# First layer of a four-layer attention kernel: two pieces of VectorE work moved to GpSimd

## The chip, the cores and the metric

The kernel runs on one core of one Trainium2 chip. The metric is the device time of one execution in microseconds (us). Engines are named as in the profile: PE is TensorE, DVE is VectorE, ACT is ScalarE, POOL is GpSimd, SP is SyncE, whose queue issues the transfers.

## The reference

Four layers run one after another on x, 8 batches of 100 rows of 512 numbers, with a context of 361 rows a batch; all in 32-bit floats. Layer 1, which the change touches, is cross-attention with grouped keys, then a residual and a norm:

```python
scores = jnp.einsum('bkgld,bksd->bkgls', q, k) * scale
attn = jax.nn.softmax(scores + mask, axis=-1)
out = out @ Wo + bo
x = out + hidden_state
return (x - mu) * jax.lax.rsqrt(var + EPS) * gamma + beta
```

Layer 2 is a recurrent mixing block that begins with a norm of x. Layer 3 is a plain attention. Layer 4 has two attentions of 16 heads of 128 columns, each with one added key `bias_k` and value `bias_v`, and a two-matrix network. The second piece of work that the change touches belongs to layer 4: the kernel does not score the added key against every query, but forms, for each head h, the product of `wq[h]` (512x128) with the row `bias_k[h] - bk[h]`. That gives a 512-vector a head, and depends on weights alone.

## The kernel before, in words

Layer 1 works through the batches b = 0 to 7 (loop from line 452). A batch has 8 x 4 x 100 rows of scores, cut into 7 row tiles t for each of 4 groups of heads. One pass of the inner loop, a *step* here, is one t: score matmuls (`scores`, L326), negated row maximum on DVE (`softmaxed`, L338), exponential on ACT (L342), transposes on PE (`turned`, L350) of the tile before, and their copies out of PSUM (`evict0`): three on ACT (L230), one on DVE (L232). In this layer the instructions of PE, DVE and ACT run in the order in which the program writes them (`manual_schedule`); those of POOL and SP are ordered by the compiler's scheduler.

Into the steps other work is woven by generators, of which `advance()` (L426) lets each go on to its next `yield` once a step:

- `values` (L378) multiplies a batch's probabilities by its values, projects them with Wo and adds the residual (L413 on POOL, L414 on DVE), then takes the row statistics (`stats`, L101 and L102).
- `finish` (L358) is the layer's end norm. It runs for the groups of batches 0 to 3, 4 and 5, and 6 and 7, when the last of a group is ready: square root on ACT (L365), reciprocal on DVE (L366), then for each batch two DVE operations (L371, L372) in one step and the statistics for layer 2 in the next. For the second and third group it also takes the square root for layer 2 (`next_ones`, L361 and L362): of batches 0 to 3, and 4 to 7. Group three runs after the loop (`while steps: advance()`, L502), with nothing else left in the layer.
- `prepare` (L143), once for each attention of layer 4, forms the added keys' vectors `wx`. It is not in that list but has one `next(adding, None)` a step from batch 1 on (L478), after the row maxima. In each step it loads the weights of one head (`wqx`, 256 KB) and its row spread over the partitions (`kb`, 64 KB), both in three buffers, and works on the head loaded two steps before: four multiply-and-sum operations on DVE at L172, one for each chunk of 128 rows. `wx` is first read in layer 4, at 880 us.

Layer 2 starts with transposes of the normed rows of batches 0 and 1 (L577), their eviction on ACT (`xu`, L579), differences on POOL (L588), and mixing on DVE (L596). There only PE's order is written by hand. Its tiles take memory that layer 1's tiles held, so its first constants (`first`, L525) are loaded when those are free. PE's spare time is filled with `fold_chunk` matmuls (`pf`).

Of the kernel before, what the change touches and what calls it, by code (L numbers as in the profile page):

```python
# [12 lines left out]
ALU = mybir.AluOpType  # L13
AX = mybir.AxisListType
PSUM = bass.MemoryType.PSUM

P = 128
B, L, C, S = 8, 100, 512, 361
T = B * L
NC = C // P  # L20
# [36 lines left out]
def kernel(ctx: ExitStack, tc: tile.TileContext, d: dict, out: bass.AP):  # L57
    nc = tc.nc
# [14 lines left out]
    mv = const.tile([L, B, 2], F32, tag="mv", name="mv")  # L73
    rstd = const.tile([L, B], F32, tag="rstd", name="rstd")
# [12 lines left out]
    x = [xpool.tile([L, C], F32, tag=f"x{b}", name=f"x{b}") for b in range(B)]  # L87
# [11 lines left out]
    def stats(pool, b, into=None):  # L99
        st = pool.tile([L, 6], F32, tag="bnst", name="bnst")  # L100
        nc.vector.bn_stats(st, x[b])  # L101
        nc.vector.bn_aggr((mv if into is None else into)[:, b, :], st)  # L102
# [33 lines left out]
    NH = 16  # L136
# [6 lines left out]
    def prepare(layer, tmp, into):  # L143


        wx = prep.tile([P, NC, NH], F32, tag=f"wx{layer}", name="wx")
        hv = tmp.tile([NH, 3, P], F32, tag="hv", name="hv", bufs=1)
        nc.sync.dma_start(out=hv, in_=d[f"L3_hv{layer}"])
        yield
        dk = hv[:, 0]  # L150
        nc.vector.tensor_tensor(dk, hv[:, 0], hv[:, 1], ALU.subtract)
        dkd = folded.tile([NH, P], F32, tag=f"dk{layer}", name="dkd")
        nc.sync.dma_start(out=dkd, in_=dk)
        nc.vector.tensor_tensor(hv[:, 1], dk, hv[:, 2], ALU.mult)
        ch = prep.tile([NH, 1], F32, tag=f"ch{layer}", name="ch")
        nc.vector.tensor_reduce(ch, hv[:, 1], AX.X, ALU.add)
        dv = prep.tile([P, NH], F32, tag=f"dv{layer}", name="dv")
        at, bt = PV_AT[f"L3_xattn_bias_v{layer}"], PV_AT[f"L3_xattn_bv{layer}"]
        nc.vector.tensor_tensor(dv, pv[:, at : at + NH], pv[:, bt : bt + NH], ALU.subtract)
        yield  # L160
        loaded = []
        for h in range(NH + 2):
            if h < NH:
                wq = tmp.tile([P, NC, P], F32, tag="wqx", name="wqx", bufs=3)
                nc.sync.dma_start(out=wq, in_=d[f"L3_xattn_wq{layer}"][h])
                kb = tmp.tile([P, P], F32, tag="kb", name="kb", bufs=3)
                nc.sync.dma_start(out=kb, in_=dkd[h : h + 1].to_broadcast([P, P]))
                loaded.append((wq, kb))
            if h > 1:
                wq, kb = loaded[h - 2]  # L170
                for c in range(NC):
                    nc.vector.tensor_tensor_reduce(  # L172
                        out=wq[:, c], in0=wq[:, c], in1=kb, scale=1.0, scalar=0.0,
                        op0=ALU.mult, op1=ALU.add, accum_out=wx[:, c, h - 2 : h - 1],
                    )
            yield
        into[layer] = wx, ch, dv

# [23 lines left out]
    with ExitStack() as es:  # L202
# [155 lines left out]
        def finish(bs):  # L358

            def next_ones(cols):  # L360
                nc.scalar.activation(rstd1[:, cols], mv1[:, cols, 1], AF.Sqrt, bias=eps5[:L], scale=1.0)  # L361
                nc.vector.reciprocal(rstd1[:, cols], rstd1[:, cols])  # L362

            cols = slice(bs[0], bs[-1] + 1)
            nc.scalar.activation(rstd[:, cols], mv[:, cols, 1], AF.Sqrt, bias=eps6[:L], scale=1.0)  # L365
            nc.vector.reciprocal(rstd[:, cols], rstd[:, cols])  # L366
            if bs == groups[1]:
                next_ones(slice(0, bs[0]))
            for b in bs:
                yield  # L370
                nc.vector.scalar_tensor_tensor(x[b], x[b], mv[:, b, 0:1], gamma, ALU.subtract, ALU.mult)  # L371
                nc.vector.scalar_tensor_tensor(x[b], x[b], rstd[:, b : b + 1], beta, ALU.mult, ALU.add)  # L372
                yield
                stats(p2, b, mv1)
            if bs == groups[2]:
                next_ones(slice(groups[1][0], bs[-1] + 1))

        def values(b, par, ats, y):  # L378
# [38 lines left out]
            for bs in groups:  # L417
                if b == bs[-1]:
                    yield from finish(bs)
# [13 lines left out]
        def added_keys():  # L433
            for layer in (1, 2):
                yield from prepare(layer, p2, added)
# [75 lines left out]
    with ExitStack() as es:  # L511
# [473 lines left out]
        with tc.manual_schedule(engines=L1_ORDERED):  # L985
# [11 lines left out]
            for n in range(NU * STEPS + 1):  # L997
                u, c, i = n // STEPS, n % STEPS // 4, n % 4
# [74 lines left out]
    with ExitStack() as es:  # L1073
# [438 lines left out]
        for n, (layer, half) in enumerate(steps):  # L1512
            wx, ch, dv = added[layer]
# [14 lines left out]
            loaded, made = [], {}  # L1528
# [253 lines left out]
```

## Time and profile before

| | |
|---|---|
| three runs | 2723.08, 2726.43, 2731.62 us; median 2726.43 |
| profiled execution: span from first to last instruction | 2722.8 us (its time is not given beside the span) |
| mean granted PE clock | 0.985 |
| busy share of the span | PE 96%, DVE 59%, POOL 38%, ACT 34% |
| layer 1, about | 0 to 311 us |
| layer 2 and 3, about | 311 to 800 us |
| layer 4, about | 800 to 2723 us |
| added keys' operations at L172 | 71.5 to 245.7 us |
| end norm at L371 and L372 | first 180.8, last 309.1 us |

A timeline line gives start, length, engine, line of the code, operation, output and inputs, shape and number. A bracket at its end is the idle time of the engine just before and what ended it. A waits line reads: engine, tile and line that waited, what it waited for, us in total, times, longest. The row of slices cuts the span into 40 equal parts; a digit is the busy share in tenths.

### The profile page before, as it was taken

Reading aid. Unit: us, or ns where it says so; the run is one execution under the profiler, and the core shown is the slowest. Engines: PE = TensorE matmul, PEld = TensorE weight load, DVE = VectorE, ACT = ScalarE, POOL = GpSimd, SP = SyncE. Lnnn points to the kernel's source line nnn. Section 1 sums busy time; section 2 is a strip of 40 time slices with the busy share of each in tenths; the row PEclk is TensorE's granted clock in tenths of the full one; section 3 lists DMA queues with packets and bytes.
Section 4 is the critical chain, followed back from the end, with each engine's and each line's share of the span. In section 5 each row is a group of like instructions: output and inputs, shape, how many; then the busy total and the mean of one; then the engine's idle time right before and its main releaser. Section 6 shows DMA issues by size and latency. Waiting matters only on the chain.

```text
span 2722.8 us, 39771 instructions
## 1 busy us (share of the span) xinstructions
PE 2609.8 (96%) x14100; PEld 2059.3 (76%) x14100; DVE 1601.2 (59%) x3987; ACT 939.2 (34%) x2143; POOL 1042.7 (38%) x1362
## 2 busy tenths in 40 slices
PE   8999889898989999999999999999999999999999
PEld 5666466676666888877789878788877788887688
DVE  4888366877524556556556556565555655654733
ACT  5777334543321333320333320243331143331211
POOL 2000144433204345455345446344446434535201
PEclk9999888999999999999999999999999999999999
DMA  7432334354214100046200034400015510005400
GB/s 230 119 104 75 115 116 124 92 145 122 81 39 151 55 23 23 4 126 169 80 23 23 1 85 145 136 16 31 12 35 151 150 43 23 23 7 168 152 13 13
DMA packets 149679, 220.58 MB, mean 81 GB/s; under 512 B 45302, under 2 KB 78646, under 8 KB 149226
## 3 DMA queue, kind: packets, MB, share of 16 engines
q1 hardware_dynamic: 149482, 218.05, 27.3%
q8 instruction: 112, 1.84, 0.3%
q14 instruction: 85, 0.70, 0.1%
HBM read 207.48 MB, written 10.53 MB: 80 GB/s over the span
## 4 chain that ended last, share of the span: by engine, by line
PE 67%; POOL 4%; DVE 3%; DMA 2%; ACT 1%; issue 1%; SPq 0%; DVEq 0%; POOLq 0%; ACTq 0%
PE pz L97 16%; PE sl L97 9%; PE pk L1175 6%; PE su L97 6%; PE pq L97 5%; PE pa L97 5%; PE po L1439 5%; PE pp L97 3%; PE pu L97 3%; PE pt L1363 2%; PE pl L97 2%; PE pl L1262 1%; DMA xin<-xd 1%; PE sc L1401 1%; PE sc L97 1%
## 5 line engine op out<-in xcount | busy, mean ns | idle before, releaser
L97 PE MATMUL pz<-at,cr 121*128 121x256 f32 (+1 forms) x960 | 255.9, 378 | 0.0
L751 POOL TENSOR_TENSOR st<-st,r 128x800 f32<-128x800 f32 x64 | 111.9, 1749 | 232.9 <-DVE st L745 198.9
L1336 DVE TENSOR_TENSOR qz<-pz,qz 128x512 f32<-128x512 f32 x192 | 131.9, 687 | 114.0 <-PE pz L97 105.8
L97 PEld LDWEIGHTS pz<-at,cr 121*128 121x128 f32 (+1 forms) x960 | 177.2, 189 | 20.8
L1175 PE MATMUL pk<-q,wb 128*128 128x400 f32 x512 | 190.2, 501 | 0.0
L97 PE MATMUL pa<-qz,wa 128*128 128x400 f32 x512 | 178.7, 500 | 0.8 <-DVE aT L1479 0.8
L97 PE MATMUL sl<-ts,ss 128*128 128x181 f32 x768 | 156.7, 326 | 3.8 <-POOL ts L1231 0.5
L97 PE MATMUL pz<-at,cs 121*128 121x256 f32 (+1 forms) x576 | 149.7, 380 | 0.0
L1248 POOL TENSOR_TENSOR ss<-qz 128x256 f32<-128x256 f32 x96 | 69.8, 727 | 203.3 <-PE su L97 115.0
L97 PEld LDWEIGHTS pa<-qz,wa 128*128 128x128 f32 x512 | 95.7, 190 | 65.9 <-DVE aT L1479 2.3
L1382 ACT ACTIVATE pr<-su,nm 128x362 f32<-128x362 f32 x96 | 54.1, 564 | 265.0 <-DVE nm L1378 264.9
L1366 ACT COPY at<-pt 121x384 f32<-121x384 f32 x192 | 84.2, 480 | 159.9 <-PE pt L1363 95.6
L1091 ACT COPY qz<-pk 128x400 f32<-128x400 f32 x128 | 63.0, 492 | 214.8 <-PE pk L1175 214.8
L97 PEld LDWEIGHTS sl<-ts,ss 128*128 128x128 f32 x768 | 118.4, 190 | 21.9 <-issue 7.1
L1175 PEld LDWEIGHTS pk<-q,wb 128*128 128x128 f32 x512 | 93.7, 190 | 45.7 <-ACT qz L1091 3.7
L745 DVE TENSOR_TENSOR_SCAN st<-wd,a 128x808 f32<-128x808 f32 x64 | 117.0, 1828 | 16.1 <-PE py L756 14.3
L350 PEld LDWEIGHTS pt<-ident,pr 115*121 115x121 f32 (+1 forms) x672 | 83.2, 185 | 56.5 <-ACT at L230 29.2
L1385 ACT ACTIVATE pr<-pr,ss 128x362 f32<-128x362 f32 x200 | 113.1, 594 | 29.1 <-DVE ss L1383 28.9
L1448 DVE TENSOR_TENSOR acc<-po,acc 128x400 f32<-128x400 f32 x196 | 111.4, 572 | 15.1 <-PE po L1439 0.5
L342 ACT ACTIVATE pr<-pr,nm 115x361 f32<-115x361 f32 (+1 forms) x224 | 115.2, 592 | 10.4 <-DVE nm L338 10.4
L97 PEld LDWEIGHTS pz<-at,cs 121*128 121x128 f32 (+1 forms) x576 | 104.4, 189 | 13.7 <-issue 1.8
L338 DVE CUSTOM_DVE_ANT_0 pr<-sc,mask 115x361 f32<-115x361 f32 (+1 forms) x224 | 106.0, 530 | 11.0 <-PE sc L326 10.4
(383 smaller groups left out, 6180.0 us busy)
## 6 DMA issues: line engine op xcount, KB each, us to landing
va<-vd SPq DMA_DIRECT2D x64, 404.0 KB
wa<-in_L_xattn_wq SPq DMA_DIRECT2D x64, 256.0 KB
wb<-in_L_xattn_wk SPq DMA_DIRECT2D x64, 256.0 KB
wa<-in_L_xattn_wv SPq DMA_DIRECT2D x64, 256.0 KB
wb<-in_L_xattn_wo SPq DMA_DIRECT2D x64, 256.0 KB
u<-pd SPq DMA_DIRECT2D x64, 200.0 KB
cr<-in_ctxR SPq DMA_DIRECT2D x16, 726.0 KB
cx<-in_ctxT SPq DMA_DIRECT2D x16, 722.0 KB
```

The source lines that it names most:

```text
L97: nc.tensor.matmul(dst, lhsT=lt, rhs=r, start=(i == 0), stop=(i == len(pairs) - 1))
L338: nc.vector.tensor_tensor_reduce(out=pr[:n], in0=sc[:n, :S], in1=mk[t][:n], scale=-1.0, scalar=FLT_MAX, op0=ALU.add, op1=ALU.min, accum_ou ...
L342: nc.scalar.activation(pr[:n], pr[:n], AF.Exp, bias=nm[:n], scale=-1.0)
L350: nc.tensor.transpose(pt[:KB, k * n : (k + 1) * n], pr[:n, lo : lo + KB], ident[:n, :n])
L745: nc.vector.tensor_tensor_scan(st.rearrange("p q b l -> p (q b l)"), wd.rearrange("p q t -> p (q t)"), a, 0.0, ALU.mult, ALU.add,)
L751: nc.gpsimd.tensor_tensor(st, st, rc.unsqueeze(1).to_broadcast([P, 4, UB, L]), ALU.mult)
L1175: nc.tensor.matmul(pk[:, :HT], lhsT=wk[:, c * P : (c + 1) * P], rhs=q, start=True, stop=True)
L1336: nc.vector.tensor_tensor(dst, pz, other, ALU.add)
L1366: nc.scalar.copy(at, pt[:KB, : 3 * TR].rearrange("p (k r) -> p k r", r=TR))
L1385: nc.scalar.activation(pr[:, : S + 1], pr[:, : S + 1], AF.Copy, scale=ss)
L1439: nc.tensor.matmul(po[:, c], lhsT=left[k][:, c * P : (c + 1) * P], rhs=right[k], start=True, stop=True)
L1448: nc.vector.tensor_tensor(acc[k], po, acc[k], ALU.add)
```

## The change

In `prepare`, POOL multiplies the whole 128 x 4 x 128 weight tile of a head by the row in one operation and folds the 128 columns to 64, 32 and 16 by additions; DVE sums the remaining 16 one step later, ahead of the next load into that buffer. So each layer's preparation takes one step more.

In `finish`, the two DVE operations of a batch become three on POOL: subtract the mean and multiply by the reciprocal deviation in one, multiply by gamma, add beta. A second `yield` leaves one step more between them and the statistics.

```diff
-        for h in range(NH + 2):
+        for h in range(NH + 3):
+            if h > 2:
+                nc.vector.tensor_reduce(wx[:, :, h - 3], loaded[h - 3][0][:, :, :16], AX.X, ALU.add)
             if h < NH:
                 wq = tmp.tile([P, NC, P], F32, tag="wqx", name="wqx", bufs=3)
                 nc.sync.dma_start(out=wq, in_=d[f"L3_xattn_wq{layer}"][h])
                 kb = tmp.tile([P, P], F32, tag="kb", name="kb", bufs=3)
                 nc.sync.dma_start(out=kb, in_=dkd[h : h + 1].to_broadcast([P, P]))
                 loaded.append((wq, kb))
-            if h > 1:
+            if 1 < h < NH + 2:
                 wq, kb = loaded[h - 2]
-                for c in range(NC):
-                    nc.vector.tensor_tensor_reduce(
-                        out=wq[:, c], in0=wq[:, c], in1=kb, scale=1.0, scalar=0.0,
-                        op0=ALU.mult, op1=ALU.add, accum_out=wx[:, c, h - 2 : h - 1],
-                    )
+                nc.gpsimd.tensor_tensor(wq, wq, kb.unsqueeze(1).to_broadcast([P, NC, P]), ALU.mult)
+                for n in (64, 32, 16):
+                    nc.gpsimd.tensor_tensor(wq[:, :, :n], wq[:, :, :n], wq[:, :, n : 2 * n], ALU.add)
             yield
...
             for b in bs:
                 yield
-                nc.vector.scalar_tensor_tensor(x[b], x[b], mv[:, b, 0:1], gamma, ALU.subtract, ALU.mult)
-                nc.vector.scalar_tensor_tensor(x[b], x[b], rstd[:, b : b + 1], beta, ALU.mult, ALU.add)
+                nc.gpsimd.tensor_scalar(
+                    x[b], x[b], mv[:, b, 0:1], rstd[:, b : b + 1], ALU.subtract, ALU.mult
+                )
+                nc.gpsimd.tensor_tensor(x[b], x[b], gamma, ALU.mult)
+                nc.gpsimd.tensor_tensor(x[b], x[b], beta, ALU.add)
+                yield
                 yield
                 stats(p2, b, mv1)
```

## The prediction

> **What bounds the kernel now.** I read the page first, for the row of slices, then the timeline of the first 320 us by batch of layer 1, then who waits for whom, then the timeline around the end of that layer.
>
> ```profile
> PE   8999889898989999999999999999999999999999
> DVE  4888366877524556556556556565555655654733
> POOL 2000144433204345455345446344446434535201
> ```
>
> One digit is 68 us. The change lies in the first four or five slices: there TensorE (PE) is at 8 or 9 tenths, VectorE (DVE) at 8 in the three in the middle, GpSimd (POOL) at nothing after the first. So there is room on GpSimd; the question is whether VectorE sets the end of anything. The busy times by stretch, cut at the start of each batch's first score matmul, say more (columns: length, PE, weight loads, DVE, ACT, POOL, granted clock, DMA share, GB/s):
>
> ```profile
> 116.50:150.90 34.40, 33.64 (x261) 22.50 (x260) 26.72 (x125) 24.37 (x56) 0.21 (x1) 1.00 0.41 117
> 150.90:186.60 35.70, 33.62 (x257) 22.41 (x256) 26.70 (x115) 27.00 (x58) 0.21 (x1) 1.00 0.33 89
> 186.60:222.00 35.40, 34.31 (x257) 22.96 (x256) 33.39 (x147) 24.40 (x55) 0.21 (x1) 1.00 0.42 118
> ```
>
> Batch 3 (first row) runs with the added keys' work inside and PE idle for 0.76 of 34.40 us. The starts of its score matmuls are 5.27, 5.21, 3.99, 6.54, 4.70, 4.60 and 4.05 us apart, and those of batches 1 and 2 the same to 0.02 us: PE's own work sets these steps, and VectorE's 26.7 us fit beside it. Only batches 4 and 5 are longer, where the end norm of batches 0 to 3 is also on VectorE. Who makes PE wait, from 40 to 250 us:
>
> ```profile
> PE pt L350 <- DVE at L232: 3.4, 6, 1.1
> PE pt L350 <- ACT at L230: 2.5, 5, 0.5
> PE pty L393 <- ACT ac L230: 0.8, 5, 0.2
> ```
>
> 3.4 us on VectorE in six waits: that is nearly all a lighter VectorE could give back here. Other stalls are hidden in matmuls that show as longer; I count those below by step lengths. At the layer's end it is different:
>
> ```profile
> 305.94 0.73 DVE L371 SCALAR_TENSOR_TENSOR x<-x,mv,gamma 100x512 f32<-100x512 f32 x1
> ...
> 309.08 0.75 DVE L372 SCALAR_TENSOR_TENSOR x<-x,rstd,beta 100x512 f32<-100x512 f32 x1
> 309.86 0.69 DVE L101 BATCH_NORM_STATS2 bnst<-x 100x6 f32<-100x512 f32 x1
> 310.59 0.18 DVE L102 BATCH_NORM_AGGREGATE mv<-bnst 100x2 f32<-100x6 f32 x1
> 310.81 0.30 ACT L361 ACTIVATE rstd<-mv,eps 100x4 f32<-100x4 f32 x1 [4.98 <-DVE mv L102]
> ...
> 311.20 1.75 ACT L579 ACTIVATE xu<-pn,pv 128x200 f32<-128x200 f32 x4
> ```
>
> This is the norm of batches 6 and 7 with nothing beside it. ScalarE (ACT) stands 4.98 us until the last statistics, takes the square root, and only then evicts layer 2's first rows (xu), which PE had finished at 305.5; PE then waits 3.21 us for xu at 312.18. The first constants of layer 2 (first, gather) are also issued only at 309.89, 0.06 us after the last use of beta. So every microsecond that this norm takes longer is late in layer 2.
>
> **The change, part by part.** *Added keys, removed:* 32 heads x 4 multiply-and-sums at L172. One is 286 ns and its read of the sum 82 ns, but they start 0.215 us apart, so 0.86 us a head, 27.5 us of VectorE in all, between 71.5 and 246 us. *Added on VectorE:* one sum of 64 elements a head. Two rows bracket it: 16 elements at 154 ns (L159) and 128 elements at 275 ns (L156); I take 0.2 us, 6.4 us in all. *Added on GpSimd:* one multiply of 512 columns (the 100x512 add of L413: 1288 ns) and folds of 256, 128 and 64 columns. 256 columns are 727 ns (L1248); the others lie between 8 columns at 248 ns (L589) and 200 at 610 ns (L1580), by the line between them 0.47 and 0.35 us. With 0.08 us between instructions, as at L1322, it is 3.1 us a head, 100 us in all, in steps that average 4.9 us. GpSimd had 0.21 us of work in a batch, so this is hidden there.
>
> What could uncover it is the ring of three buffers. Now it is load, sum, next load, once in three steps; after the change it is load, multiply and fold, sum, next load, also once in three steps. A load is issued at 96.40 (wqx) and 96.80 (kb) and the DMA share falls to 0.05 within 3 us; so the ring needs 0.2 for the sum, 0.8 for the issues, 3 for landing, 3.1 on GpSimd and about 0.3 for hand-overs (an estimate from the gaps of these rows): 7.4 us. Three neighbouring steps last at least 13.26 us (5.26, 5.22 and 2.78 in batch 6). 5.9 us are to spare, and a norm of 3.3 us ahead in GpSimd's queue fits in them too. If the cover went, the VectorE sum would wait in order ahead of the copies at L232, for which PE waits; that is the second rival.
>
> *End norm, removed:* 8 x (746 + 752 ns) of VectorE, 12 us. *Added on GpSimd:* one subtract-and-multiply and two 100x512 tensor operations a batch. The first is bounded by 679 ns (L1471, 128x400, same kind) from below and 1288 ns (L413) from above; scaled from L1471 it is 0.81. The others go by L413, eight in 9.92 us, 1.24 each. 3.3 us a batch. Each norm of batches 0 to 5 then has two steps, at least 8.0 us (2.78 + 5.22), before its statistics, so on GpSimd it is hidden; the square root that needs batches 0 to 3 comes 13 steps after the first norm, and the last of these statistics 11. No DMA is moved, and the mask loads on SP keep their places behind loads that are not late.
>
> *What the lighter VectorE gives.* I compare the steps of batches 4 to 6 with the undisturbed ones: 4.47 for 4.05; 5.35 for 5.27, 5.53 for 5.22, 6.66 for 6.54, 5.15 for 4.60; 2.97 for 2.78. Excess 0.42 + 0.08 + 0.31 + 0.12 + 0.55 + 0.19 = 1.7 us, all in steps with a norm or its statistics next to a head's sums. I count it as gained. Two more steps are long, 5.59 for 4.60 and 5.78 for 4.60; there VectorE stands 1.33 and 1.24 us for a square root for which ScalarE first loads a table (1.28 us). The change leaves that load, so these 2.2 us stay. Bounds: 0, and 1.7 + 2.2 = 3.9 us.
>
> *What the end norm costs.* Before: from 305.94 to 309.83, 3.9 us for batches 6 and 7 with the statistics of 6 between. After: GpSimd 2 x 3.3 = 6.6 us, the statistics of 6 beside it, 0.1 for crossing engines: 2.8 us later. Bounds: the lowest of all rows, 2 x (0.68 + 2 x 1.24) = 6.3, so +2.4; and GpSimd slowed as by VectorE at L648 against L834 (1879 against 1522 ns, 128x800 both), 6.6 x 1.235 = 8.15, so +4.3. Nothing hides it: xu, the constants and the fold matmuls all come after it.
>
> The Trainium skill, GPSIMD Engine Reference, section 4.1 Engine selection, speaks against this part: it says that two-input elementwise work belongs on VectorE, being about twice as slow on GpSimd, with one-input work near line rate. By twice L371 and once L371 a batch would be 0.75 + 2 x 1.49 = 3.7 us, an estimate, and the delay 3.5 instead of 2.8 us.
>
> The Trainium skill, GPSIMD Engine Reference, section 2.1 Instruction dispatch, says that the first call of a freshly loaded kernel costs about 6 us that no instruction shows; no run here shows it for this operation, whose first use would fall on batch 0's norm.
>
> *Sum.* -1.7 + 2.8 = **+1.1 us**. The profiled span is 2722.8 us, 0.3 below the shortest of the three runs (2723.08) and 3.6 below their median; no separate time of that execution is shown. From the span it would be 2723.9; against the median of 2726.43 it is 2727.5, and that is my number. A comparison of this kernel cannot tell less than about 0.3% (8.2 us) from no change, so I call it no change.
>
> **Rivals.** *One: a chain reaction in layer 2 (slower or faster).* That layer is a chain across engines; the granted clock is 0.89 from 305 to 320 us and 0.74 from 320 to 340, against 1.00 before. If PE's longer wait costs one more such 20 us stretch, 0.26 x 20 = 5.2 us come on top of 1.1; two would give +11.5, 2738. The same could go the other way: all of PE's waits in the loop (3.4 + 2.5 + 0.8 = 6.7 us) and one such stretch saved give 2714.5. For: only PE's order is fixed in that layer, and L766 takes 394 to 1912 ns by what lies beside it. Against: nearly everything in it hangs on the same late release and shifts as a whole.
>
> *Two, the slower side: GpSimd sets the ring.* It decides when landing exceeds 13.26 - 4.4 = 8.9 us, or GpSimd's share of the ring exceeds 13.26 - 4.3 = 9.0 us: then VectorE waits at each sum and a step lasts a third of the ring. At a ring of 17.6 us a step would be 5.9 instead of 4.9, and 32 steps cost +31 us: 2758. For: GpSimd in order also has a clearing at L288, which waits for VectorE once a batch. Against: the 3 us of landing, and no instruction waits for wqx or kb now.
>
> *Three: the layer's end is hidden.* If ScalarE evicts xu ahead of the last square root, the 2.8 us go and -1.7 is left: 2724.7. Against: the constants are held by beta all the same.
>
> **Chances.** Forecast (+1.1, within -1.5 and +4.3, with the runs' scatter 2720 to 2735): 0.61. Rival three: 0.09, also no change. Rival one 0.22, of it 0.09 faster by over 0.3%, 0.10 slower, 0.03 neither. Rival two 0.08, slower. Faster 0.09, same 0.73, slower 0.18. The range 2715 to 2742 takes in the forecast and both signs of rival one and leaves most of rival two and the far tails out.
>
> **What would show it.** Right: steps of batches 1 to 3 unchanged to 0.05 us; the steps of batches 4 and 5 at 5.27, 5.22, 6.54 and 4.6 but the two with table loads still long; VectorE some 33 us less busy and GpSimd some 126 us more; the last square root at L361 some 2.8 us later after the last reciprocal, and xu right behind it. Wrong: a VectorE sum that waits for GpSimd; score steps longer than PE's work; or layer 2 longer or shorter by more than the 3 us with which it starts, which would be rival one.

## The result, and the profile after

The change makes the kernel slower: 2762.52 us (median of 6 runs, 2752.46 to 2765.64) against 2731.28 us for the kernel before beside it (6 runs, 2723.08 to 2739.68), a ratio of 1.0113 with a 95% interval of 1.0096 to 1.013. The prediction was 2727.5 us, no change, with a range up to 2742. The profiled execution has a span of 2750.7 us and a time of 2752.46, so 1.8 us lie outside the span; its granted clock is 0.977 (0.985 before).

The row of slices of the changed kernel, from its page:

```profile
PE   8998889888989999999999999999999999999999
DVE  4665346887623556556565555655555655654733
POOL 2455234443202345446345546344536434545301
```

GpSimd has now work in the first five slices and VectorE has less, as planned; TensorE has not become fuller. Layer 1 in parts, by the start of the first score matmul, the last residual add and the first eviction of layer 2 (`xu`):

| us | before | after | |
|---|---|---|---|
| loop: first score to last residual add | 284.63 | 300.79 | +16.2 |
| end: last residual add to first xu | 7.34 | 12.67 | +5.3 |
| rest: first xu to the last instruction | 2411.6 | 2417.3 | +5.6 |
| span | 2722.8 | 2750.7 | +27.8, of it 0.7 before the first score |

In the changed code the VectorE sum is L164, the load of a head's weights (wqx) L167, of its row (kb) L169, GpSimd's multiply L173 and folds L175, the norm L371, L374 and L375; later lines are 4 higher than before. The loop by batch, the busy times from one batch's first score matmul to the next (columns as before: length, PE, weight loads, DVE, ACT, POOL, granted clock, DMA share, GB/s):

```profile
117.24:153.52 36.28, 33.86 (x258) 22.53 (x257) 22.28 (x83) 24.45 (x55) 19.53 (x29) 1.00 0.44 123
153.52:189.12 35.60, 33.89 (x257) 22.53 (x256) 22.40 (x83) 27.21 (x59) 16.69 (x19) 1.00 0.30 80
189.12:230.51 41.39, 37.13 (x257) 25.32 (x257) 23.02 (x84) 24.76 (x56) 24.63 (x29) 0.92 0.28 78
```

These are batches 3, 4 and 5. VectorE is lighter in each of them, and batch 4 even gains 0.1 us, but batch 3 takes 1.9 and batch 5 takes 6.0 us longer, and in batch 5 the granted clock is 0.92 where it was 1.00. Batch 6, not shown, takes 8.7 us longer. VectorE is not too busy there; it waits. The waits view from 40 to 305 us says for whom:

```profile
POOL wqx L173 <- DMA wqx<-in_L_xattn_wq: 56.4, 16, 9.0
DVE wx L164 <- POOL wqx L175: 33.9, 15, 4.6
...
PE pt L350 <- DVE at L232: 13.1, 7, 3.1
```

Read it from the bottom: PE waits 13.1 us (3.4 before) for the copies at L232; these stand in VectorE's order behind the sum at L164, which waits 33.9 us for GpSimd's folds; and GpSimd is not slow but stands 56.4 us in 16 waits for weights. So a transfer is late. Why it is late is seen in SP's queue (timeline of SP alone):

```profile
224.67 0.33 SPq L169 DMA_DIRECT2D kb<-dkd  x1
225.09 0.37 SPq L313 DMA_DIRECT2D mask<-in_mask_Bx1xSxS_ff  x1
225.55 0.33 SPq L167 DMA_DIRECT2D wqx<-in_L_xattn_wq  x1
```

and in GpSimd's and VectorE's timelines at the same place:

```profile
223.38 1.27 POOL L173 TENSOR_TENSOR wqx<-wqx,kb 128x512 f32<-128x512 f32 x1 [3.96 <-DMA wqx<-in_L_xattn_wq]
224.72 1.65 POOL L175 TENSOR_TENSOR wqx<-wqx 128x256 f32<-128x256 f32 x3
229.52 1.28 POOL L173 TENSOR_TENSOR wqx<-wqx,kb 128x512 f32<-128x512 f32 x1 [3.15 <-DMA wqx<-in_L_xattn_wq]
```

```profile
226.41 0.22 DVE L164 TENSOR_REDUCE wx<-wqx 128x4 f32<-128x64 f32 x1 [3.63 <-POOL wqx L175]
226.54 0.56 DVE L232 COPY ac<-av 128x400 f32<-128x400 f32 x1
227.02 0.51 DVE L232 COPY at<-pt 121x345 f32<-121x345 f32 x1
```

Counting the loads from the start, the row issued at 224.67 is the 27th and the weights issued at 225.55 are the 25th. Row 27 takes the buffer of row 24, which is free when the multiply of head 24 ends: 224.65. Only behind it in SP's order comes the load of weights 25, which the *next* multiply needs. It is issued at 225.55 and that multiply starts at 229.52. The loop closes there: multiply, row load, mask, weights load, landing, multiply, about 6.1 us for each head (multiplies at 223.38, 229.52, 235.72, 241.61), where steps average 4.9. The three buffers are still there, but only one head's weights are in flight.

Before, a head's row and weights were freed by the same instruction, the last sum at L172, and the scheduler kept the two loads together (timeline of SP alone, kernel before):

```profile
230.99 0.35 SPq L165 DMA_DIRECT2D wqx<-in_L_xattn_wq  x1
231.39 0.42 SPq L167 DMA_DIRECT2D kb<-dkd  x1
```

After the change kb is free after the multiply, the weights' buffer only after the VectorE sum, and the scheduler, which orders SP's queue, put each row two heads ahead of the weights.

At the end of the layer (timeline of all engines):

```profile
323.03 4.13 POOL L371 TENSOR_SCALAR x<-x,mv,rstd 100x512 f32<-100x512 f32 x2 [43.79 <-DVE rstd L366]
...
327.13 2.48 POOL L374 TENSOR_TENSOR x<-x,gamma 100x512 f32<-100x512 f32 x2
329.56 2.48 POOL L375 TENSOR_TENSOR x<-x,beta 100x512 f32<-100x512 f32 x2
330.86 0.69 DVE L101 BATCH_NORM_STATS2 bnst<-x 100x6 f32<-100x512 f32 x1 [7.94 <-POOL x L375]
...
333.02 0.30 ACT L361 ACTIVATE rstd<-mv,eps 100x4 f32<-100x4 f32 x1 [10.30 <-DVE mv L102]
...
333.42 1.74 ACT L583 ACTIVATE xu<-pn,pv 128x200 f32<-128x200 f32 x4
```

One subtract-and-multiply takes 2.08 us (all eight between 2075 and 2087 ns), not 0.81, and the scheduler interleaves the two batches, so even the first statistics start only at 330.86, 1.2 us before the last addition ends. The same interleaving puts the norms of batches 0 to 3 on GpSimd in one block, from 180.63 to 198.74 us.

### The profile page after: what moved, and what is told of

Read it like the earlier page. It is cut to its first block, busy times and chain, and to the rows that moved or that the text cites. A ratio compares the mean times of both kernels' runs of the same rounds, so it can differ in the third digit from the quotient of the medians.

```text
span 2750.7 us, 39704 instructions
## 1 busy us (share of the span) xinstructions
PE 2628.2 (96%) x14100; PEld 2074.1 (75%) x14100; DVE 1569.3 (57%) x3747; ACT 939.9 (34%) x2143; POOL 1166.7 (42%) x1514
## 4 chain that ended last, share of the span: by engine, by line
PE 68%; POOL 3%; DVE 3%; DMA 1%; ACT 1%; issue 1%; SPq 0%; DVEq 0%; POOLq 0%; ACTq 0%
PE pz L97 16%; PE sl L97 9%; PE pk L1179 6%; PE pa L97 6%; PE su L97 5%; PE pq L97 5%; PE po L1443 5%; PE pp L97 3%; PE pu L97 3%; PE pt L1367 2%; PE pl L97 2%; PE pl L1266 1%; PE sc L1405 1%; PE sc L97 1%; POOL ss L1252 1%
## 5 line engine op out<-in xcount | busy, mean ns | idle before, releaser
L350 PEld LDWEIGHTS pt<-ident,pr 115*121 115x121 f32 (+1 forms) x672 | 84.7, 187 | 65.7 <-ACT at L230 26.8
L350 PE MATMUL pt<-ident,pr 115*121 115x115 f32 (+1 forms) x672 | 102.1, 283 | 19.5 <-DVE at L232 13.1
```

What stands on the lines that cost most here:

```text
L350: nc.tensor.transpose(pt[:KB, k * n : (k + 1) * n], pr[:n, lo : lo + KB], ident[:n, :n])
```

## The experiments

**Theory A**: SP's order of the loads makes the ring serial, and that is the loss in the loop; the end's loss is the norm's own length. **Rival B**: the norms, a block of 18 us in GpSimd's order, make the folds late, and the ring would be well without them. **Rival C**: three buffers are too few, whatever the order. Parts are given as in the table above.

One piece of the loop has to be told apart. From the last score matmul to the last residual add, the same work has two lengths, with two granted clocks, here in the kernel before and in the fourth experiment (columns as above):

```profile
284.15:303.86 19.71, 17.15 (x85) 8.64 (x84) 4.62 (x15) 7.28 (x15) 0.00 (x0) 0.91 0.04 15
282.87:300.83 17.96, 15.47 (x85) 8.13 (x84) 4.62 (x15) 7.28 (x15) 0.00 (x0) 1.00 0.04 16
```

VectorE and ScalarE are busy for the same time in both; only the clock and PE differ. The short form also came in the second, fifth and sixth experiments and in one of the three profiles of the changed kernel, the long one in all the others. So these 1.75 us are not to be put down to an edit, and where a run has the short form its loop is given up to the last score matmul as well.

### Added keys alone

The norm is back on VectorE, as before; the added keys' part is as in the change.

```diff
-                nc.gpsimd.tensor_scalar(
-                    x[b], x[b], mv[:, b, 0:1], rstd[:, b : b + 1], ALU.subtract, ALU.mult
-                )
-                nc.gpsimd.tensor_tensor(x[b], x[b], gamma, ALU.mult)
-                nc.gpsimd.tensor_tensor(x[b], x[b], beta, ALU.add)
-                yield
+                nc.vector.scalar_tensor_tensor(x[b], x[b], mv[:, b, 0:1], gamma, ALU.subtract, ALU.mult)
+                nc.vector.scalar_tensor_tensor(x[b], x[b], rstd[:, b : b + 1], beta, ALU.mult, ALU.add)
```

> The changed kernel with its end norm put back on VectorE, so only the added keys are on GpSimd. Theory A (the ring of loads is made serial by SP's queue, where the row kb of the head three further on stands ahead of the next head's weights wqx; 6 us a head against steps of 4.9): the last residual add of layer 1 (L414 of before, at 303.9 us) comes 8 to 16 us later than in before, VectorE's sums wait for GpSimd as in the changed kernel, the time is 8 to 22 us over before. Rival B (the 18 us block of four end norms in GpSimd's queue is what made the folds late): the last residual add comes at most 3 us later, the sums hardly wait, the time is within 8 us of before.

Measured: loop 292.67 (+8.0), the last residual add 7.7 us later (just under the 8 to 16 expected), end 7.34 (as before), span 2735.5; 2739.79 us against 2727.46, ratio 1.0051 (1.0035 to 1.0068). The waits view of this kernel, from 40 to 305 us:

```profile
POOL wqx L173 <- DMA wqx<-in_L_xattn_wq: 59.2, 15, 10.2
...
DVE wx L164 <- POOL wqx L175: 19.2, 8, 4.0
```

The sum waits 19.2 us in 8 waits, for heads 11 to 14 and 27 to 30, with no norm on GpSimd at all. So rival B is not the cause by itself; it can only add to it.

### End norm alone

The added keys' part is as before, the norm as in the change.

```diff
-                nc.gpsimd.tensor_tensor(wq, wq, kb.unsqueeze(1).to_broadcast([P, NC, P]), ALU.mult)
-                for n in (64, 32, 16):
-                    nc.gpsimd.tensor_tensor(wq[:, :, :n], wq[:, :, :n], wq[:, :, n : 2 * n], ALU.add)
+                for c in range(NC):
+                    nc.vector.tensor_tensor_reduce(
+                        out=wq[:, c], in0=wq[:, c], in1=kb, scale=1.0, scalar=0.0,
+                        op0=ALU.mult, op1=ALU.add, accum_out=wx[:, c, h - 2 : h - 1],
+                    )
```

> Before with only the end norm moved to GpSimd. Both theories: the steps of layer 1 as in before to 1 us, the end of the layer (last reciprocal to the first eviction of xu) 5.3 us longer as in the changed kernel, because the subtract-and-multiply takes 2.08 us and the two batches are interleaved. Time 4 to 12 us over before, the part above 5.3 by the granted clock after it. If layer 2 absorbs a late start, the time is within 3 us of before.

Measured: loop 285.33 (+0.7; up to the last score matmul +2.5), end 12.66 (+5.3), span 2730.9; 2732.06 us against 2727.46, ratio 1.002 (1.0011 to 1.003). The end's loss is the norm's alone. The loop did not stay as it was: two multiply-and-sums at L172 took 1.36 and 1.34 us instead of 0.286, and their step 8.36 us instead of 5.35; the fifth experiment shows with what that goes together.

### The whole change, with row and weights in one buffer

The row is a fifth slice of the weights' tile, so both are free at the same moment, after the sum. Again three buffers.

```diff
-                wq = tmp.tile([P, NC, P], F32, tag="wqx", name="wqx", bufs=3)
+                both = tmp.tile([P, NC + 1, P], F32, tag="wqx", name="wqx", bufs=3)
+                wq, kb = both[:, :NC], both[:, NC]
...
-                kb = tmp.tile([P, P], F32, tag="kb", name="kb", bufs=3)
```

> The changed kernel whole, but weights and row of a head lie in one buffer, so that no row can be loaded ahead of the sum that frees it. Theory A: SP's queue has both loads of a head together, the ring takes some 7.5 us in three steps, the sums do not wait but near the four norms; the last residual add is 1 us earlier to 3 us later than in before; the end of the layer still 5.3 us longer; time 4 to 12 us over before. Rival B: the 18 us of norms still make the folds late, the last residual add comes 10 us or more late, time 18 to 30 us over before.

Measured: loop 286.11 (+1.5), end 12.65 (+5.3), span 2733.4; 2734.95 us against 2727.46, ratio 1.0033 (1.002 to 1.0046). The sum waits once, behind the block of norms (waits view from 40 to 305 us):

```profile
DVE wx L164 <- POOL wqx L175: 4.6, 1, 4.6
```

That step is 8.00 instead of 3.98 us, and the next gives 1.0 back; then GpSimd does three heads in 9 us and has caught up. This is rival B by itself: one step, 4.0 us. With the serial ring GpSimd does not catch up, since each next head is again 6.1 us away: in the changed kernel each sum of heads 20 to 30 waits, with keys alone only those of heads 27 to 30. So 8.0 us (keys alone) became 16.2.

### Added keys alone, one buffer

Both edits above: the norm on VectorE, and row and weights in one tile.

> Added keys on GpSimd with weights and row in one buffer, end norm on VectorE as before. Theory A: the sums never wait, the last residual add 0 to 1.7 us earlier than in before (the step excess that the prediction counted), end of the layer as before, time 3 us under to 2 us over before. Rival B says the same here.

Measured: loop 282.29 (-2.3; up to the last score matmul -0.6), end 7.35, span 2725.0; 2728.75 us against 2727.46, ratio 1.0009 (0.9997 to 1.002). No sum waits for GpSimd any more. SP's queue (timeline of SP alone):

```profile
224.72 0.35 SPq L168 DMA_DIRECT2D wqx<-in_L_xattn_wq  x1
225.13 0.42 SPq L169 DMA_DIRECT2D wqx<-dkd  x1
```

Weights and row of one head stand together again, as in the kernel before. The loss is gone. Of the -2.3 us, 1.75 are the clock of the last stretch; the lighter VectorE, which here keeps the norm, gains 0.6.

### The norm's first operation as multiply and add

The norm alone, as in the second experiment, with (x - m) r written as x r + (-m r); VectorE forms -m r for a group in one 0.16 us operation.

```diff
+            nc.vector.scalar_tensor_tensor(mv[:, cols, 0], mv[:, cols, 0], -1.0, rstd[:, cols], ALU.mult, ALU.mult)
...
-                    x[b], x[b], mv[:, b, 0:1], rstd[:, b : b + 1], ALU.subtract, ALU.mult
+                    x[b], x[b], rstd[:, b : b + 1], mv[:, b, 0:1], ALU.mult, ALU.add
```

> As the run with only the end norm on GpSimd, but its first operation written as multiply by the reciprocal deviation and add of the negative scaled mean (one small VectorE operation a group makes that), the form of L1471 in before. If the form sets the price, the operation takes 0.8 to 0.9 us instead of 2.08, and from the last residual add to the first xu it is 10.2 to 10.5 us instead of 12.66 (7.34 in before): the 2.8 us that the prediction counted. If it is the shape or writing in place, 2.0 us and 12.6 us stay. Time 1 to 7 us over before.

Measured: this operation takes 769 ns instead of 2074, and the end 10.25 instead of 12.66 us (+2.9 over before). The loop is 287.54 (+2.9; up to the last score matmul +4.7), span 2729.8; 2736.26 us against 2727.41, ratio 1.0028 (1.0016 to 1.004), 8.9 us over before and so outside the 1 to 7 that were expected. So against the second experiment the end gains 2.4 us and the loop loses 2.2, and nothing is left of the cheaper operation. Where the loop lost it, by VectorE's and GpSimd's timelines:

```profile
181.08 1.35 DVE L172 CUSTOM_DVE_ANT_0 wqx<-wqx,kb 128x128 f32<-128x128 f32 x1
182.37 0.08 DVE L172 DVE_READ_ACCUMULATOR2_ANT wx<- 128x1 f32 x1
182.37 1.35 DVE L172 CUSTOM_DVE_ANT_0 wqx<-wqx,kb 128x128 f32<-128x128 f32 x1
```

```profile
178.24 1.52 POOL L372 TENSOR_SCALAR x<-x,rstd,mv 100x512 f32<-100x512 f32 x2 [21.57 <-DVE mv L367]
179.72 2.56 POOL L375 TENSOR_TENSOR x<-x,gamma 100x512 f32<-100x512 f32 x2
182.25 2.58 POOL L376 TENSOR_TENSOR x<-x,beta 100x512 f32<-100x512 f32 x2
```

While GpSimd runs its two-input operations, of 1.28 us each, the multiply-and-sum on VectorE takes 1.35 us instead of 0.286 (in the kernel before none took over 290 ns), one for each operation of GpSimd. The row maxima between them, which read one operand from PSUM, stay at 0.52. Six of the eight multiply-and-sums that start from 180.3 to 191.5 us took 1.33 to 1.36 (only two did in the second experiment), and PE waited 2.82 us at L350 behind the first of them. The Trainium skill, SBUF — State Buffer, section Who interferes with whom, says that a VectorE instruction with two SBUF inputs contends with a GpSimd instruction that reads SBUF, and calls the port pair that they share an exclusive lock. These rows agree with it; no run here takes GpSimd's operations away and leaves the rest as it is.

### Added keys alone, the row's load on another queue

As the first experiment, with the rows' loads issued from ScalarE. Separate buffers, three each.

```diff
-                nc.sync.dma_start(out=kb, in_=dkd[h : h + 1].to_broadcast([P, P]))
+                nc.scalar.dma_start(out=kb, in_=dkd[h : h + 1].to_broadcast([P, P]))
```

> Added keys alone on GpSimd, three buffers each for weights and row as in the change, but the row's load is issued from ScalarE's queue, in program order, so it cannot stand ahead of the next weights in SP's. Theory A (SP's order makes the ring serial): VectorE's sums no longer wait, first score to last residual add 281 to 284 us (284.6 in before, 292.7 with the row on SP), time within 4 us of before. Rival C (three buffers are too few for load plus GpSimd work): still 290 us or more, time 8 us or more over before.

Measured: loop 282.98 (-1.7; up to the last score matmul +0.1), end 7.35, span 2724.6; 2726.34 us against 2727.41, ratio 0.9992 (0.9976 to 1.0007). No sum waits for GpSimd. Three buffers with separate releases are enough once the row no longer stands ahead of the weights in the same queue: rival C falls, and theory A holds by a second way of mending it.

### Everything mended

One buffer as in the third experiment; norms of batches 0 to 5 on GpSimd as multiply and add; those of batches 6 and 7, beside which nothing runs, on VectorE as before.

```diff
+                if bs == groups[2]:
+                    nc.vector.scalar_tensor_tensor(x[b], x[b], mv[:, b, 0:1], gamma, ALU.subtract, ALU.mult)
+                    nc.vector.scalar_tensor_tensor(x[b], x[b], rstd[:, b : b + 1], beta, ALU.mult, ALU.add)
+                else:
+                    nc.gpsimd.tensor_scalar(
+                        x[b], x[b], rstd[:, b : b + 1], mv[:, b, 0:1], ALU.mult, ALU.add
+                    )
```

> What the theory recommends: added keys on GpSimd with weights and row in one buffer, the end norm of batches 0 to 5 on GpSimd in the multiply-and-add form, that of batches 6 and 7 on VectorE as in before. Theory A: first score to last residual add 281 to 285 us, end as in before (7.3 us), time 5 us under to 1 us over before. Rival B (norms in GpSimd's queue make folds late): the loop is 3 us or more longer than before, as one step of 8.0 us in the run with one buffer and all norms shows.

Measured: loop 283.18 (-1.5), end 7.35, span 2724.5; 2727.81 us against 2727.41, ratio 0.9999 (0.9987 to 1.001). The last stretch is the long one here, as in the kernel before, so the 1.5 us are gained in the steps. The whole loss is gone, and there is no gain that the medians can show: 1.5 us in 2727 are 0.05%.

### The same kernels once more

The loop and the end explain 22.2 us with the 0.7 ahead of the first score, the medians differ by 31.2. To see which part varies, the changed kernel was profiled twice more and the kernel before once more, unaltered.

> The changed kernel unaltered, profiled once more, to see which of its parts vary from one execution to the next. The serial queue order fixes a loop of layer 1 of 300.8 us (first score to last residual add) and an end of 12.7 us: if these explain all, both come out again within 1 us, and what varies is the time from xu to the end (2417.3 us in the first profile), by several us with the half-clock stretches. The other theory: the loop itself varies, because waits of PE lower the granted clock at other places in each execution; then it comes out anywhere from 295 to 310 us, and the medians' difference of 31 us has its remainder there.

> The changed kernel unaltered, a third profile, with the same expectations: loop 300.8 and end 12.7 within 1 us if queue order alone sets them; a loop between 295 and 310 us if the granted clock in it differs from one execution to the next.

> The kernel before unaltered, a second profile, as the measure for the two above. Its loop has hardly any wait of PE: 284.6 us again within 0.5 us by both theories, end 7.3 us; the rest (2411.6 us in the first profile, which is near the fastest of its runs) some 3 to 8 us longer if the rest is what varies in every kernel.

| us | loop | end | rest | span |
|---|---|---|---|---|
| after, first profile | 300.79 | 12.67 | 2417.3 | 2750.7 |
| after, second | 304.28 | 12.66 | 2411.0 | 2748.3 |
| after, third | 300.61 | 12.67 | 2420.0 | 2753.0 |
| before, first | 284.63 | 7.34 | 2411.6 | 2722.8 |
| before, second | 284.63 | 7.35 | 2412.3 | 2723.6 |

Both happen. The changed loop is no fixed number: 16.0 to 19.7 us over before (16.1 to 21.4 up to the last score matmul), with long steps that differ from one execution to the next (the sixth step of batch 3 is 6.51, 8.46 and 6.40 us), while the kernel before repeats to 0.01 us. And the rest varies by 9 us, in layers whose code the change does not touch. The rest of the kernel before varies too, since its runs spread from 2722 to 2739 us, though its two profiles hit the low end; the 3 to 8 us more that were expected of the second did not come (0.6).

## Why the prediction was wrong

*The ring, the step that failed.* The working summed one head's way through its buffer, 7.4 us in three steps, and found that "5.9 us are to spare". Each term held: landing with its issue took 4.0 us, GpSimd's share 3.0 us a head (1275, 728, 456 and 319 ns, against 1288, 727, 470 and 350 taken), the sum 0.22. What failed is the sentence "No DMA is moved, and the mask loads on SP keep their places behind loads that are not late". The loads of wqx and kb are themselves instructions in an order, and the change gave their buffers different releasers. The sum assumed that each load is issued when its own buffer is free; it was issued when the load ahead of it in the queue could be. Three loads in flight became one, and the measure was no longer 7.4 against 13.3 us for three heads, but 6.1 against 4.9 for one. Keys alone cost +8.0 us in the loop; up to the last score matmul they cost +8.1, and -0.6 or +0.1 when mended in either of two ways.

*Rival two* described what happened downstream to the letter: a sum that waits, ahead of the copies at L232 for which PE waits. Its conditions were wrong. It asked for a landing over 8.9 us or a GpSimd share over 9.0, and neither was needed.

*The norm in GpSimd's queue.* A norm of 3.3 us was to fit into the spare time, each by itself, three steps apart in the program. The scheduler owns GpSimd's order in this layer; it made a block of 18.1 us. In a ring that can catch up this costs one step, 4.0 us (third experiment). On top of the serial ring it raised 8.0 to 16.2.

*The end norm, right in kind and wrong in size.* That it lies bare, and that xu follows the last square root directly, held. +2.8 was predicted with a bound of +4.3, and +5.3 measured. The mis-sized term is the subtract-and-multiply: 0.81 us, scaled from a row of the same kind of instruction, with 1.29 as the upper bound; it measured 2.08. (How 0.81 was scaled is not told; in proportion to the columns it would be 0.87. The bounds +2.4 and +4.3 also leave out the 0.1 us for crossing engines that the +2.8 has.) Written as multiply and add it took 0.77 and the end cost +2.9, so the rest of that sum was right. The step that failed is to take L1471 for the same kind. The profile's row gives only the instruction's name; in the code that line multiplies and adds, and the change subtracts and multiplies.

The rule of the Trainium skill that the prediction weighed (GPSIMD Engine Reference, section 4.1 Engine selection) would have made a batch 3.7 us, an estimate; 2.08 + 2 x 1.28 = 4.6 us were measured, and 0.77 + 2 x 1.28 = 3.3 with multiply and add. Of a first call's extra 6 us (the same page, section 2.1 Instruction dispatch) the trace shows nothing: GpSimd starts the first norm 0.1 us after the reciprocal that it waits for ends, and it takes 2.08 us like the others.

*The lighter VectorE, about right.* The -1.7 us were counted in six steps. The run that tests them is the last one, where the keys and the norms of batches 0 to 5 are off VectorE and nothing covers the gain: these six became 1.28 us shorter, and the loop up to the last score matmul 1.4. The -2.3 and -1.7 of the fourth and sixth experiments come near the forecast by luck: most of them is the clock of the last stretch. Of the six, the step of 2.97 (0.19) was misread: it begins after the last head's sums, at 245.7 us, and stayed as long in the last run. The steps with table loads stayed long, as said (5.58 to 5.70 and 5.77 to 5.86 in these three runs). VectorE is 31.9 us less busy (33 predicted), GpSimd 124.0 more (126).

*Steps of batches 1 to 3.* Those of 1 and 2 are unchanged to 0.01 us. In batch 3 the sums of heads 11 to 13 wait 0.84, 1.13 and 2.60 us and no step is longer for it; that of head 14 waits 3.41 us, and its step is 6.51 instead of 4.60.

*What stays open.* The medians differ by 31.2 us. Of these 16 to 20 are the loop, 5.3 the end. The remaining 6 to 10 lie in the rest, in runs of the loop worse than the three profiled, or in the scatter of six runs: the three profiled executions took 2752.46, 2750.12 and 2754.80 us, all under the median, and the kernel before came to medians of 2727.46 and 2727.41 in the 20 and 29 runs beside the experiments. Waits of PE with a lower granted clock behind them are seen in the loop (0.92 in batch 5); that such waits also move the clock of the later layers, which rival one had in mind, was not shown: the rest of the changed kernel came out at -0.7, +5.6 and +8.4 us against the kernel before's first profile, and both of its profiles are from the low end of its own spread.

## What to carry to other kernels

When a change gives two tiles that are loaded together different last readers, write down the order of their loads in the issuing queue and ask, for each load, what the one ahead of it waits for: a ring is as deep as that order allows, not as deep as its buffers. Keeping both in one tile, or in two queues, cost nothing that could be measured and removed the whole loss of the ring here. And a stage with no other work beside it is the last place from which to move work to a slower engine, however idle that engine is.

## What the runs showed of the hardware

- On GpSimd the same instruction on 100 x 512 numbers takes 2074 ns as subtract and multiply and 769 ns as multiply and add. Its two-input operations on the same shape lie between, at 1.27 to 1.31 us (medians of the rows in the second and fifth experiments).
- A VectorE multiply-and-sum with both inputs in SBUF goes from 0.286 to 1.35 us beside GpSimd's two-input operations; the sum of one input (L164) took 215 to 222 ns in the changed kernel, also where GpSimd's multiply ran beside it.
- In the changed kernel's loop the granted clock fell to half in or behind PE's waits of 2.13, 3.12 and 2.12 us, not behind those of 1.66 and 1.28. Around the wait of 3.12 us that ends at 235.07 us (stretches before, with and after it):

```profile
227.00:230.00 3.00, 2.42 (x18) 2.42 (x18) 2.34 (x10) 1.81 (x4) 0.48 (x1) 1.00 0.45 137
229.50:235.00 5.50, 2.46 (x20) 1.58 (x18) 2.37 (x8) 2.27 (x6) 2.77 (x4) 0.86 0.33 90
235.00:240.50 5.50, 5.43 (x26) 5.43 (x27) 2.05 (x10) 2.39 (x5) 2.78 (x4) 0.52 0.27 76
```

The clock (third number from the end) goes from 1.00 to 0.52, and PE is busy throughout the last stretch. So such a wait costs more than its own length: in batch 5 the same matmuls keep PE busy for 37.13 us instead of 34.31. A wait of that size is not needed: in the last stretch of the loop no wait reaches 1 us, and a half-clock stretch of 3.4 us came in seven of the twelve profiles.
